# Two first part products of each single-row point placed ahead of the first softmax turns, the third ones behind

## The chip, the cores and the metric

The kernel runs on one core of one Trainium2 chip. The metric is the device time of one execution in microseconds (us), taken as the median of several runs.

## The reference, cut to what matters

The input `x` is four images of 256 channels by 64 by 64, in float32. Layer 0 computes 49 logits for every pixel, makes a softmax of them and uses the result as the weights of a 7x7 window with dilation 2. Layer 1 whitens the channels in four groups of 64 with statistics over all images.

```python
k = conv(x, w1, padding=6, rhs_dilation=2) + b1          # 128 channels, 7x7
k = conv(k, w2) + b2                                     # 49 logits per pixel
attn = softmax(k, axis=1)
shifts = stack([xp[:, :, 2*u:2*u+64, 2*v:2*v+64] for u in range(7) for v in range(7)])
x = einsum('bkchw,bkhw->bchw', shifts, attn)             # weighted 7x7 window
# layer 1: mean and covariance per group of 64 channels, five Newton steps for the
# inverse root, then the whitening matrix applied to the centred x, gain and shift
```

## The kernel before, in words

**The convolution.** The two convolutions of layer 0 are folded into one 7x7 filter bank with 49 outputs (`tap`). It is computed by interpolation in both directions: rows are taken in groups of four phases and combined at seven row points (`row_eval`), columns likewise at seven column points (`col_eval`), the products of one row point with all column points are matmuls (`conv_bank`, line 604) into two PSUM buffers `cv0` and `cv1` used in turn, and the results are interpolated back (`col_interp`, `row_interp`). Rows of one parity of one image lie in one of five SBUF slots, `slot0` to `slot4`. Logits of the first image lie in the first part of `slot4`.

Two of the seven row points, 0 and `INF`, need a single row phase, so their products may be made directly from the input with the seven column taps (`direct`, line 779, or in three part products). For the second image both points are made from three part products over pairs of columns (`direct_part`, line 862): part 2 uses the even taps, part 1 the odd taps, and part 3 uses sums of neighbouring taps on sums of neighbouring columns. `direct_sums` makes these sums on VectorE (line 345 is the helper that records every addition, lines 348 and 352 the ones for subtractions and multiply-adds), `direct_ends` joins the parts in `zz`: ScalarE copies part 1 (line 885), VectorE adds part 2 twice and subtracts the joined value from part 3. Point `INF` uses the PSUM buffers `acc0`, `acc1` and a `cv` buffer; point 0 uses two `cv` buffers and `acc0` (`direct_start`). Its taps are in the tile `lgx`, which later holds the weights of another row point (loaded by SyncE, line 426) and then logits.

**The weighted window of the first image.** `softmax(0, 0)` turns the logits by eight transposes on TensorE (line 1135), takes maxima on VectorE (line 1171), sixteen exponentials on ScalarE (line 1175), then scales and shuffles on VectorE (lines 1150 to 1159 and 1123). `move_terms` lets ScalarE copy the result into `zt` (line 1253) and GpSimd write it to DRAM (`sd`, line 1272). `load_band` lets SyncE read it back as a band matrix (`band`, line 1322). Then `weighted_sum` (line 1442) multiplies the band with turned blocks of the image (`xb`, transposes of line 1378). A second softmax, `softmax(0, 1)`, serves the other column parity.

**The order.** Each engine works through its own queue in order. A scheduler lays the instructions of each engine in an order from the program's order and priorities; during the first image the VectorE operations of the helpers are also chained one behind the other (`in_turn`, line 322). At the border between the images the program says

```python
    prepare(NR0, 0)                      # row and column point values of image 1
    xs, ws = direct_sums(1, INF, [w], gbr...)
    direct0(5, 1)
    row_interp(0, 1)                     # last logits of image 0
    direct_part(1, INF, 2, ...); direct_part(1, INF, 1, ...); direct_part(1, INF, 3, ...)
    prepare(NR0, 1); prepare(NR0, 2)
```

and then, for image 1, the steps `soft(0, 0)`, `direct_start(0)` (parts 2 and 1 of point 0), `direct_start(1)` (part 3 of point 0), `soft(0, 1)`, and the first `conv_step`s, which contain the first weighted sums at marked places.

Of the kernel before, what the change touches and what calls it, by code (L numbers as in the profile page):

```python
# [9 lines left out]
F32 = mybir.dt.float32  # L10
# [13 lines left out]
INF = 6  # L24
# [8 lines left out]
def kernel(  # L33
# [29 lines left out]
    nc = tc.nc  # L63
    B, C, H, W = x.shape
    P = 128
    NCC = C // P
    O1 = w1.shape[0]
    KT = w2.shape[0]
    KS = 7
# [12 lines left out]
    Q8 = SH // 4  # L82
# [23 lines left out]
    ps_y = ctx.enter_context(tc.tile_pool(name="ps_y", bufs=2, space=bass.MemoryType.PSUM))  # L106
# [74 lines left out]
    t = tp()  # L181
# [3 lines left out]
    t = tp()  # L185
# [5 lines left out]
    for k in range(2):  # L191
        t = ps_cv.tile([P, 512], F32, name=f"cv{k}")
# [8 lines left out]
    UPOS = {u: k for k, u in enumerate((6, 4, 5, 3, 2, 0, 1))}  # L201
    gpool = tc.alloc_tile_pool(name="gp", bufs=1, side="right")
    tap = gpool.tile([P, KS, KS, NCC, KT], F32, name="tap")
    gbr = gpool.tile([P, KS, NCC, 2, KT], F32, name="gbr")
# [33 lines left out]
    lgx = const.tile([P, max(SH * W, n3)], F32, name="lgx")  # L238
    gr0 = lgx[:, :n0].rearrange("p (v a s k) -> p v a s k", v=KS, a=NCC, s=2)
# [6 lines left out]
    for k, c0 in enumerate(range(0, P, CB)):  # L246
        n = min(CB, P - c0)
        t = cv_buf[k % 2]
# [15 lines left out]
    for k0 in range(0, KT, TB):  # L264
        n = min(TB, KT - k0)
        t = tp()
# [36 lines left out]
    spare = pv[:, NV - 1].rearrange("p n q b -> p (n q b)")  # L303
# [40 lines left out]
    def add(o, a, b):  # L344
        return in_turn(TT(o, a, b, ALU.add))  # L345
# [381 lines left out]
    def row_interp(b, part):  # L727

        pt = {k: zz[:K2, k] for k in range(NP)}
        lg = lgx  # L730
        if b == 0:
            lg = store[4].rearrange("p c r w -> p (c r w)")
        lg = lg[:, : SH * W].rearrange("p (r w) -> p r w", w=W)
        outs = phases(lg[:K2])
        cut = lambda t, k: t[:, k : k + Q8]
        tr = ct.rearrange("p a b -> p (a b)")[:K2, : Q9 * W].rearrange("p (q w) -> p q w", w=W)
        interpolate(pt, tr, outs, cut, part)
        if part == 0:
            done_ = ((0, outs[0]), (2, outs[2]))
        else:  # L740
            done_ = ((3, cut(pt[5], 0)), (1, outs[1]))
            logits[b] = lg
        for a, t in done_:

            def end(a=a, t=t):
                return nc.scalar.activation(outs[a], t, AF.Identity, bias=bias[:K2])

            if b > 0 and part == 0:
                later.append(end)
            else:  # L750
                end()
# [51 lines left out]

    M16, NX = W // 4, Q8 * 2 * NCC * W // 2

    def direct_sums(b, br, w, room):

        a = 3 if br == INF else 0
        xs = []
        for h in range(2):  # L810
            x = slots[2 * b + h].rearrange("p c r w -> p (c r w)").rearrange(
                "p (e a w) -> p a e w", a=4, w=SW
            )
            x = x[:, a].rearrange("p e (m i two) -> p i e m two", i=2, two=2)
            o = room[:, h * NX // 2 : (h + 1) * NX // 2]
            add(o.rearrange("p (e m two) -> p e m two", m=SW // 4, two=2), x[:, 0], x[:, 1])
            xs.append(
                o.rearrange("p (c g q w) -> p c g q w", c=NCC, g=2, q=Q8).rearrange(
                    "p c g q (m two) -> p c g q m two", two=2
                )  # L820
            )
        ws = []
        for s, t in enumerate(w):
            nw = (KS // 2) * NCC * KT
            o = room[:, NX + s * nw : NX + (s + 1) * nw]
            o = o.rearrange("p (v a k) -> p v a k", v=KS // 2, a=NCC)
            for j in range(KS // 2):
                add(o[:, j], t[2 * j + 1], t[2 * j])
            ws.append([o[:, j] for j in range(KS // 2)] + [t[KS - 1]])
        return xs, ws  # L830

    def direct_part(b, br, part, ps, w, xs=None):

# [42 lines left out]
    def direct_view(ps, n, m):  # L876
        return ps.rearrange("p q w -> p (q w)")[:, : n * m * 2].rearrange(
            "p (q m two) -> p q m two", q=n, two=2
        )

    def direct_ends(br, n, p1, p2, p3=None):

        z = zz[:K2, br, :n].rearrange("p q (m i two) -> p i q m two", i=2, two=2)
        if p3 is None:
            nc.scalar.copy(z[:, 0], p1[:K2])
            add(z[:, 1], z[:, 0], p2[:K2, :, 1:])
            add(z[:, 0], z[:, 0], p2[:K2, :, :M16])
        else:
            sub(z[:, 1], p3[:K2], z[:, 1])
# [3 lines left out]
    def conv_psum():  # L893
        ncv[0] += 1
        return cv_buf[(ncv[0] - 1) % 2].rearrange("p (q w) -> p q w", w=W)

    def direct_inf(b):
# [2 lines left out]
        t = spare[:, :NTAP].rearrange("p (v a k) -> p v a k", v=KS, a=NCC)  # L900
        direct(b, INF, 0, conv_psum(), [t[:, v] for v in range(KS)])

    start_of = {}

    def direct_start(sr):

        n = Q8 + 1
        w = [[gr0[:, v, :, s] for s in range(2)] for v in range(KS)]
        if sr == 0:
            room = store[4].rearrange("p c r w -> p (c r w)")[:, SH * W :]  # L910
            xs, ws = direct_sums(1, 0, [[t[s] for t in w] for s in range(2)], room)
            start_of["xs"] = xs
            start_of["ws"] = [[t[j] for t in ws] for j in range(KS // 2 + 1)]
            p2 = direct_view(conv_psum(), n, M16 + 1)
            direct_part(1, 0, 2, p2, w)
            p1 = direct_view(conv_psum(), n, M16)
            direct_part(1, 0, 1, p1, w)
            direct_ends(0, n, p1, p2)
        else:
            p3 = direct_view(acc[0], n, M16)  # L920
            direct_part(1, 0, 3, p3, start_of["ws"], start_of["xs"])
            direct_ends(0, n, None, None, p3)

    acc = [ps_y.tile([P, Q8, W], F32, tag="y", name=f"acc{sr}") for sr in range(2)]
    for a in acc:
        nc.vector.memset(a, 0.0)
    rows = [(0, br) for br in (1, 2, 3)]
    NR0 = len(rows)
    rows += [(b, br) for b in range(1, B) for br in ROWS if b > 1 or br]
# [41 lines left out]
    def direct0(br, sr):  # L971
        if br in xrs:
            gb = gb5 if br == 5 else gbr
            direct(
                0, br, sr, conv_psum() if br == 5 else acc[sr],
                [gb[:, v, :, sr] for v in range(KS)], xrs[br],
            )
        else:
            u = KS - 1 - 4 * sr - (3 if br == INF else 0)
            w = [tap[:, UPOS[u], v] for v in range(KS)]  # L980
            direct(0, br, sr, conv_psum() if br == INF else acc[sr], w)
# [92 lines left out]
    col_interp(0, 3)  # L1074
    row_interp(0, 0)
    prepare(NR0, 0)
    w = [tap[:, UPOS[3], v] for v in range(KS)]
    xs, ws = direct_sums(1, INF, [w], gbr.rearrange("p v a s k -> p (v a s k)"))
    direct0(5, 1)
    row_interp(0, 1)  # L1080

    w = [[t] for t in w]
    p2 = direct_view(acc[0], Q8, M16 + 1)
    direct_part(1, INF, 2, p2, w)
    p1 = direct_view(acc[1], Q8, M16)
    direct_part(1, INF, 1, p1, w)
    p3 = direct_view(conv_psum(), Q8, M16)
    direct_part(1, INF, 3, p3, [[t] for t in ws[0]], xs)
    prepare(NR0, 1)
    prepare(NR0, 2)  # L1090
    strict[0] = False
    direct_ends(INF, Q8, p1, p2)
    direct_ends(INF, Q8, None, None, p3)
    gpool.release()


# [563 lines left out]
    def soft(b, pc):  # L1660
        steps = softmax(b, pc)

        def step():
            with tc.high_priority() if pc == 0 else nullcontext():
                next(steps, None)

        step()
        if b == 0:
            step()
            if pc == 0:  # L1670
                bands(0)
        else:
            rest_of.append(step)
# [32 lines left out]
    for b in range(1, B):  # L1706

        steps = []
        for k, (bk, br) in enumerate(rows):
            if bk == b:  # L1710
                for i, cost in enumerate((6, 5, 2)):
                    steps.append((cost, lambda k=k, i=i: conv_step(k, i)))
        if b == 1:
            for sr in range(2):
                steps.insert(sr, (12, lambda sr=sr: direct_start(sr)))
            steps.insert(0, (0, lambda: soft(0, 0)))
            steps.insert(3, (0, lambda: soft(0, 1)))
        else:
            steps.insert(0, (12, lambda b=b: direct_inf(b)))
        j, at, whole = 0, 0, sum(c for c, _ in steps)  # L1720
        for cost, f in steps:
            half_next[0] = (at + cost) * NPC >= (j + 1) * whole and (b, j) in half_gaps
            f()
            while rest_of:
                rest_of.pop()()
            at += cost
            if at * NPC >= (j + 1) * whole:
                gap(b, j)
                j += 1
                while after_gap:  # L1730
                    after_gap.pop()()
# [26 lines left out]
    n = 4 * last_b  # L1758
# [186 lines left out]
    pair = bank_pairs()  # L1945
# [88 lines left out]
```

## Time and profile before

| | |
|---|---|
| median of 3 runs | 668.89 us (668.85 to 669.1) |
| the profiled execution | 668.98 us |
| its span in the trace | 667.2 us |
| TensorE (PE) busy | 638.7 us, 96% |
| VectorE (DVE) busy | 571.2 us, 86% |
| ScalarE (ACT) busy | 331.8 us, 50% |
| GpSimd (POOL) busy | 115.3 us, 17% |
| mean granted TensorE clock | 0.991 |

The profile has one execution. A busy time counts instructions on an engine. The chain of waits follows the work that ended last back to the beginning, step by step, to what released it. In rows of the timeline the first column is the start, the second the busy time, `x` the number of instructions, and a bracket holds the idle time just before and what ended it. Consecutive instructions overlap a little at their ends, so the distance from one start to the next is shorter than the busy time of one.

### The profile page before, as it was taken

How to read it: one execution, taken by the hardware profiler on the slowest of the kernel's cores; microseconds unless marked ns; L12 is line 12 of the kernel's file. 1: busy time of each engine (PE TensorE's matmuls, PEld its weight loads, DVE VectorE, ACT ScalarE, POOL GpSimd, SP SyncE). 2: the span in 40 equal slices, each digit the busy share in tenths (PEclk: the TensorE clock that was granted, in tenths of full speed). 3: DMA queues.
4: the chain of work that ended last, by engine and by line, in shares of the span. 5: the costliest groups of instructions: out<-in, count | busy, mean ns of one | idle time of the engine just before them, and what ended most of it. 6: DMA issues, size and time to landing. Idle time of an engine off the chain costs nothing.

```text
span 667.2 us, 19415 instructions
## 1 busy us (share of the span) xinstructions
PE 638.7 (96%) x7992; PEld 530.1 (79%) x7992; DVE 571.2 (86%) x1258; ACT 331.8 (50%) x861; POOL 115.3 (17%) x173
## 2 busy tenths in 40 slices
PE   6999999999999999999999999999999999999991
PEld 1439673358999998889999998999999999997440
DVE  3699999999899889999999799989999988634781
ACT  1434331013565566467754554473855667535681
POOL 0000551663213002001022020002220203500000
PEclk9999999999999999999999999999999999999996
DMA  8961799995599988324588673026364325739698
GB/s 316 247 177 67 128 232 382 218 195 83 133 205 223 228 257 304 103 57 108 149 278 278 232 246 107 1 69 195 103 197 112 70 65 129 182 96 380 263 412 335
DMA packets 109840, 126.11 MB, mean 189 GB/s; under 512 B 69127, under 2 KB 92216, under 8 KB 107576
## 3 DMA queue, kind: packets, MB, share of 16 engines
q1 hardware_dynamic: 92952, 69.35, 35.5%
q0 software_dynamic: 10752, 37.26, 21.7%
q10 hardware_dynamic: 6048, 18.27, 8.8%
q8 instruction: 63, 1.03, 0.7%
q14 instruction: 25, 0.20, 0.1%
HBM read 78.78 MB, written 52.36 MB: 197 GB/s over the span
## 4 chain that ended last, share of the span: by engine, by line
PE 62%; DVE 17%; issue 7%; POOL 4%; SPq 4%; DMA 3%; ACT 2%; DVEq 0%; ACTq 0%; POOLq 0%
PE cv L604 25%; PE y L1442 13%; PE sig L1533 5%; PE tp L1514 4%; PE tp L1378 4%; SPq L225 4%; POOL ahead L147 2%; POOL slot L147 2%; PE tp L1844 2%; PE cv L862 2%; DVE zz L352 2%; DVE rb L345 2%; PE cv L779 2%; DVE xh L352 2%; DVE pv L352 1%
## 5 line engine op out<-in xcount | busy, mean ns | idle before, releaser
L604 PE MATMUL cv<-xh,wr 128*49 128x128 f32 x4160 | 232.3, 273 | 0.1
L604 PEld LDWEIGHTS cv<-xh,wr 128*49 128x49 f32 x4160 | 226.2, 124 | 2.9 <-issue 1.0
L1272 POOL DMA_DIRECT2D sd<-zt x120 | 63.3, 534 | 292.2 <-ACT zt L1253 222.2
L1442 PE MATMUL y<-band,xb 128*128 128x209 f32 x448 | 93.7, 341 | 0.6 <-ACT xb L1409 0.6
L1442 PEld LDWEIGHTS y<-band,xb 128*128 128x128 f32 x448 | 75.7, 191 | 1.5 <-ACT xb L1409 0.8
L615 ACT COPY pv<-cv 113x486 f32<-113x486 f32 (+2 forms) x60 | 25.9, 431 | 82.4 <-PE cv L604 82.2
L352 DVE SCALAR_TENSOR_TENSOR pv<-pv 113x162 f32<-113x162 f32 x176 | 52.5, 320 | 1.5 <-ACT pv L615 1.0
L1524 ACT COPY yt<-tp 128x512 f32<-128x512 f32 x60 | 35.0, 591 | 24.3 <-PE tp L1514 23.5
L1253 ACT COPY zt<-d 32x112 f32<-32x112 f32 (+2 forms) x132 | 38.6, 293 | 11.0 <-DVE d L1123 5.1
L1514 PE MATMUL tp<-ident,slot 128*128 128x128 f32 x240 | 41.3, 295 | 0.2 <-ACT slot L1464 0.2
L1378 PE MATMUL tp<-ident,slot 128*128 128x128 f32 x256 | 40.5, 282 | 0.0
L1175 ACT ACTIVATE d<-tp,mx 128x49 f32<-128x49 f32 x96 | 27.4, 321 | 24.2 <-DVE mx L1172 17.6
L1533 PE MATMUL sig<-yt 128*64 128x65 f32 x1024 | 38.0, 225 | 0.9 <-ACT yt L1524 0.9
L1514 PEld LDWEIGHTS tp<-ident,slot 128*128 128x128 f32 x240 | 34.9, 205 | 5.0 <-issue 3.7
L1378 PEld LDWEIGHTS tp<-ident,slot 128*128 128x128 f32 x256 | 38.2, 204 | 0.2 <-issue 0.2
L1533 PEld LDWEIGHTS sig<-yt 128*64 128x64 f32 x1024 | 32.9, 137 | 6.7 <-issue 1.9
L1409 ACT COPY xb<-tp 128x512 f32<-128x512 f32 x52 | 30.6, 588 | 13.7 <-PE tp L1378 10.5
L352 DVE SCALAR_TENSOR_TENSOR xh<-ct 128x512 f32<-128x512 f32 x40 | 26.6, 691 | 5.7 <-PE cv L604 5.4
L147 POOL DMA_DIRECT2D slot<-in_x_dram x12 | 20.4, 1701 | 53.4 <-DVE xh L352 38.6
L348 DVE TENSOR_TENSOR pv<-pv 113x162 f32<-113x162 f32 (+1 forms) x77 | 27.5, 364 | 0.3
L352 DVE SCALAR_TENSOR_TENSOR xh<-xh,rb 128x512 f32<-128x512 f32 x40 | 27.4, 684 | 0.1
L345 DVE TENSOR_TENSOR ct<-rb 128x1024 f32<-128x1024 f32 (+1 forms) x26 | 26.5, 1020 | 0.3
(288 smaller groups left out, 1141.9 us busy)
## 6 DMA issues: line engine op xcount, KB each, us to landing
band<-sd SPq DMA_DIRECT2D x64, 242.0 KB, 3.6
sd<-zt POOLq DMA_DIRECT2D x120, 77.0 KB, 4.2
wr<-gd ACTq DMA_DIRECT2D x14, 588.0 KB, 4.8
wr<-gd ACTq DMA_DIRECT2D x14, 490.0 KB, 4.1
slot<-in_x_dram POOLq DMA_DIRECT2D x12, 512.0 KB, 10.5
ahead<-in_x_dram POOLq DMA_DIRECT2D x12, 512.0 KB, 7.8
spill<-slot POOLq DMA_DIRECT2D x3, 2048.0 KB, 9.4
slot<-ahead POOLq DMA_DIRECT2D x3, 2048.0 KB, 10.7
```

Of the source, the lines that this page charges most:

```text
L147: yield queue.dma_start(o[:, cc, h], src[:, :, pr, h * SW : (h + 1) * SW])
L345: return in_turn(TT(o, a, b, ALU.add))
L352: return in_turn(STT(o, a, f, b, ALU.mult, ALU.add))
L604: nc.tensor.matmul(o, wv[:, sc, sr, cc], xv[bc][:, h * NCC + cc], start=(j == 0), stop=(j == len(terms) - 1), skip_group_check=True,)
L1253: ins = nc.scalar.copy(o, i)
L1272: dma = queue.dma_start(bass.AP(tensor=D.tensor, offset=D.offset + h * HS + g * RS, ap=[[LS, TC], [CR * RS, NCH], [1, KS * WS]],), zt[p0 : ...
L1378: nc.tensor.transpose(t[:, h * C + cc * P : h * C + (cc + 1) * P], tile_of(xt, cc, t8, h, pc), turned_by(n),)
L1409: (nc.vector.tensor_copy if n > 4 * B - 3 else nc.scalar.copy)(xb.rearrange("p a c -> p (a c)"), t[:, : 2 * C])
L1442: nc.tensor.matmul(y_ps[n, half, cc][:, q0 : q0 + nq, c0:c1], xb[:, cc * P : (cc + 1) * P], rhs, start=(k == 0), stop=(k == len(PIECES[hal ...
L1514: nc.tensor.transpose(t[:, h * C + cc * P : h * C + (cc + 1) * P], tile_of(yt, cc, t8, h, pc), turned_by(n),)
L1524: return nc.scalar.copy(yb.rearrange("p h a g c -> p (h a g) c")[:, :, :GW], t[:, : 2 * C].rearrange("p (e c) -> p e c", c=GW),)
L1533: nc.tensor.matmul(sig[g * GW : (g + 1) * GW, cc], yb[:, g, :GW], yb[:, g], start=(count[0] == 0), stop=end, skip_group_check=True,)
```

## The change

The three part products of `INF` are taken apart: parts 2 and 1 are joined as soon as they are made, part 3 is made in `direct_start(1)`, just ahead of part 3 of point 0. `direct_start(0)` now stands ahead of `soft(0, 0)`. Point 0's part 3 goes to `acc1` instead of `acc0`, so one `cv` buffer less is drawn and the two change places from there on. The column sums of `INF` go to `spare` (a part of `pv`), its tap sums and a copy of its last tap (ScalarE) to the free end of `lgx`. The sums of the taps are made in one addition over all of them, where there were three for `INF` and six for point 0.

```diff
+        return xs, direct_taps(w, sums)
+
+    def direct_taps(w, sums):
+        n = w.shape[2]
+        o = sums[:, : KS // 2 * n].rearrange("p (v n) -> p v n", n=n)
+        pair = w[:, : KS - 1].rearrange("p (v two) n -> p two v n", two=2)
+        add(o, pair[:, 1], pair[:, 0])
+        return [o[:, j] for j in range(KS // 2)] + [w[:, KS - 1]]
...
         else:
-            p3 = direct_view(acc[0], n, M16)
+            third_inf()
+            p3 = direct_view(acc[1], n, M16)
             direct_part(1, 0, 3, p3, start_of["ws"], start_of["xs"])
             direct_ends(0, n, None, None, p3)
+    def third_inf():
+        p3 = direct_view(acc[0], Q8, M16)
+        direct_part(1, INF, 3, p3, start_of["ws_inf"], start_of["xs_inf"])
+        direct_ends(INF, Q8, None, None, p3)
...
     prepare(NR0, 0)
-    w = [tap[:, UPOS[3], v] for v in range(KS)]
-    xs, ws = direct_sums(1, INF, [w], gbr.rearrange("p v a s k -> p (v a s k)"))
     direct0(5, 1)
+    p2 = direct_view(acc[0], Q8, M16 + 1)
+    direct_part(1, INF, 2, p2, [one(g[:, v]) for v in range(KS)])
+    p1 = direct_view(acc[1], Q8, M16)
+    direct_part(1, INF, 1, p1, [one(g[:, v]) for v in range(KS)])
     row_interp(0, 1)
-    w = [[t] for t in w]
-    p2 = direct_view(acc[0], Q8, M16 + 1)
-    direct_part(1, INF, 2, p2, w)
-    p1 = direct_view(acc[1], Q8, M16)
-    direct_part(1, INF, 1, p1, w)
-    p3 = direct_view(conv_psum(), Q8, M16)
-    direct_part(1, INF, 3, p3, [[t] for t in ws[0]], xs)
+    direct_ends(INF, Q8, p1, p2)
+    room = lgx[:, 2 * KS * NCC * KT :]
+    start_of["xs_inf"], ws = direct_sums(1, INF, g, spare, room)
     prepare(NR0, 1)
     prepare(NR0, 2)
     strict[0] = False
-    direct_ends(INF, Q8, p1, p2)
-    direct_ends(INF, Q8, None, None, p3)
+    last_tap = room[:, KS // 2 * NCC * KT :][:, : NCC * KT]
+    nc.scalar.copy(last_tap, g[:, KS - 1])
...
             for sr in range(2):
                 steps.insert(sr, (12, lambda sr=sr: direct_start(sr)))
-            steps.insert(0, (0, lambda: soft(0, 0)))
+            steps.insert(1, (0, lambda: soft(0, 0)))
             steps.insert(3, (0, lambda: soft(0, 1)))
```

## The prediction

> **What bounds the kernel now.** I read the page first: the engines, then the shares of the chain that ended last.
>
> ```profile
> PE 638.7 (96%) x7992; PEld 530.1 (79%) x7992; DVE 571.2 (86%) x1258; ACT 331.8 (50%) x861; POOL 115.3 (17%) x173
> PE 62%; DVE 17%; issue 7%; POOL 4%; SPq 4%; DMA 3%; ACT 2%; DVEq 0%; ACTq 0%; POOLq 0%
> ```
>
> PE is nearly always busy, so only PE idle time can be won. Next, PE's waits from 150 to 320 us: two lie in the changed stretch.
>
> ```profile
> PE tp L1135 <- ACT slot L746: 1.6, 1, 1.6
> PE cv L862 <- DVE gbr L345: 0.9, 1, 0.9
> ```
>
> The first is the turn of the first logits, the second the third product of `INF`, waiting for its sums. Then the chain of waits from 140 to 215 us:
>
> ```profile
> 154.16 0.73 ACT slot L746
> 154.89 0.04 issue
> 154.94 1.21 PE tp L1135 x8
> 156.15 12.56 PE cv L862 x218
> 168.71 6.56 PE acc L862 x128
> 175.27 0.68 PE tp L1378 x4
> 175.95 0.95 PE tp L1135 x8
> 176.90 9.74 PE cv L604 x176
> 186.64 0.91 PE y L1442 x4
> ```
>
> From the turns to the first weighted sum (line 1442, starting at 186.57 in the timeline) PE never waits, and the chain stays on PE to 247 us. But the sum also needs the band, so I followed the band in the timelines of DVE, ACT and SP:
>
> ```profile
> 149.74 0.61 DVE L345 TENSOR_TENSOR zz<-zz,cv 113x448 f32<-113x448 f32 x1
> 155.91 1.03 DVE L1171 TENSOR_REDUCE mx<-tp 128x8 f32<-128x392 f32 x2
> 166.84 3.33 ACT L1253 COPY zt<-d 128x56 f32<-128x56 f32 x11 [5.11 <-DVE d L1123]
> 176.94 0.91 SPq L1322 DMA_DIRECT2D band<-sd x2
> 176.45 1.05 DVE L1171 TENSOR_REDUCE mx<-tp 128x8 f32<-128x392 f32 x2 [0.16 <-PE tp L1135]
> ```
>
> Maxima begin at 155.91 and the band load at 176.94, which is 21.0 us of latency. The load's issues to landing are 3.65 us, so the band is there at 180.6: 6.0 us of slack before 186.57. The last row shows the other thing to see: DVE's first stop of any size after 140 us is at 176.3. Until then it works without a pause, so an operation's time there is its place in DVE's queue.
>
> **The change on PE.** `INF`'s first two parts end at 148.86 as before. Point 0's parts 2 and 1 need only taps and input, so they follow at once: 148.86 + 12.56 = 161.4. The logits are ready long before, so the turns take 0.95 (row 175.95, without the idle start): 162.4. `INF`'s third part takes 3.5 (149.80 to 153.29 in PE's timeline): 165.9. Point 0's third 6.56: 172.4. Transposes and second turns 0.68 + 0.95, convolution 9.74: PE stands before the first weighted sum at 183.8. That is 2.8 us earlier than 186.57: the waits of 0.94 and 1.65 and 0.26 of the idle start. This is the whole gain on offer.
>
> **The change on DVE.** In the changed program's queue the maxima of the first softmax no longer follow the last logit operations; the sums for the third parts and much of the next rows' preparation stand ahead. From 148.02, where DVE began `INF`'s column sums, the queue now holds, by start-to-start distances of the same rows before:
> - last logits, from the `zz` addition to the last multiply-add into the logits (149.74 to 154.05): 4.3
> - the two additions of part 2 of `INF`: 2 x 0.4 = 0.8
> - `INF`'s column sums: 1.2 (148.02 to 149.23); its tap sums, one addition of 294 elements, like 113x288 (0.36 to 0.45): 0.4
> - `ct` and the `xh` of two banks (1.25, 0.61, 0.60, 0.72, 1.34): 4.5
> - point 0's column sums: 1.2; its tap sums, one addition of 588, like 113x576 (0.67 to 0.76): 0.7
> - `rb` 2.20, `rb` 1.13, `ct` 1.14: 4.5
>
> The sum is 17.6, so the maxima begin at 165.6 against 155.91: 9.7 later, though their turns are ready at 162.4. The single tap additions save about 0.1 for `INF` (0.51 for three) and 0.4 for point 0 (six at 0.17 to 0.25); this is in the sum.
>
> **The band.** After the maxima come the exponentials, 1.2 later, for 4.6, at 171.4. Meanwhile DVE does `zz` additions, three `rb` steps of 1.14 and the subtraction of `INF`'s third part. That subtraction is a new wait on PE ahead of the reciprocals, hence ahead of the whole band; its product ends at 165.9 and DVE reaches it at 169.6, so it costs nothing, and would cost only what the product ran past 169.6. Reciprocals to shuffles take 1.7 after the exponentials (184.01 against 182.3 in the second softmax; 1.87 in the first). So the shift shrinks to 9.5. Copies, GpSimd's writes and SyncE's load follow as before (10.1 us from the first copy to the load): load at 186.45, landed at 190.1. **PE, ready at 183.8, waits 6.3 us and starts the sum at 190.1 instead of 186.57: +3.5.** The gain of 2.8 is turned into a wait.
>
> **Queues passed.** On SP the load of `spare` (126.54 before) now waits for `INF`'s third product, 165.9, and stands ahead of the `lgx` load (175.32 before, now 172.4) and the band: both go before 186.45, cost 0. ACT's copy of part 1 stands ahead of the exponentials: done at 161.9, needed at 166.8, cost 0; without that cover it is 0.43. The copy of the last tap, 98 elements, lies before 130 us, where ACT is mostly idle: 0, at most 0.3. POOL keeps its order. On ACT the second softmax's sixteen exponentials, behind the late `zt` copies, run 180.1 to 184.8 instead of 177.67 to 182.3, and DVE waits for them about 4 us. What is queued behind on DVE (`xh`, `pv`) then ends near 195; the next `xh` needs the convolution behind the weighted sums, which ends at 197, so the delayed sums hide it.
>
> **Landing.** Two weight loads (588 and 490 KB, ACT queue) now start at about 184.8 and 185.4, just ahead of the band. Band loads took 2.4 to 8.1 us over the trace, median 3.6; the next pair, issued with a weight load beside it, took 7.5. I take 3.65, because the first pair had the 686 KB load of `lgx` 1.6 us ahead of it as well. The bounds are -1.2 and +4.5.
>
> **The clock.** No idle time of 6 us inside this trace shows its price. The end does: PE's last matmul ends at 652.85, and the windows table (the clock is the third number from the right) gives
>
> ```profile
> 652.00:654.00 2.00, 0.85 (x8) 0.00 (x0) 1.54 (x2) 1.58 (x3) 0.00 (x0) 1.00 0.99 401
> 654.00:656.00 2.00, 0.00 (x0) 0.00 (x0) 0.00 (x0) 0.00 (x0) 0.00 (x0) 0.90 0.98 410
> 656.00:658.00 2.00, 0.00 (x0) 0.00 (x0) 0.00 (x0) 0.00 (x0) 0.00 (x0) 0.50 1.06 442
> ```
>
> A mean of 0.90 over 2 us is full clock until 655.6, then half: the clock falls about 2.75 us after the last matmul. An idle time of 6.3 us should see it fall. How long it stays low afterwards no row shows. It cannot gain; at most the first weighted sums and their transposes (186.57 to 191.5) run at half rate, +5.0. I take the fall time for the return too: 2.75 us at half rate lose 1.4. The Trainium skill, TensorE: Matmul & The Clock Gate, Part 1, speaks against a change that opens such a gap: it halves the clock after an idle window of about 3.4 us and restores it after about as long a busy one. By that page, as an estimate, the loss would be 1.7 instead of 1.4.
>
> **Sum.** +3.5 + 1.4 = +4.9, all on PE's chain, which passes it on: to 247 us the chain is PE, then DVE released by PE (its waits there name `PE cv L604`), then PE again. The profiled execution took 668.98 us (span 667.2 and 1.8 around it), 0.09 above the median. 668.98 + 4.9, rounded: 673.9.
>
> **Rivals.** (1) The band is hidden and PE's gaps are simply closed: 668.98 - 2.8 = 666.2. It needs the band shifted by no more than 183.8 - 180.6 = 3.2 us; the turns alone come 162.4 - 156.15 = 6.3 later, which speaks against it. 5%. (2) DVE does not hold the maxima back (its queue runs shorter than the rows): the shift is that of the turns, 6.3 to 6.5, the band lands at 187.0, and PE starts 0.5 later than before, with an idle time of 3.2 at the edge of the clock's fall: 669.5, no change. It decides if DVE reaches the maxima by 162.5; 17.6 us of rows would have to shrink by 3. 9%. (3) The band lands in 7.5 beside the weight loads: +3.85 more, 677.8. 15%. (4) The clock does not fall, or returns at once: +3.5, 672.5; I count it to the forecast's range.
>
> **How the numbers follow.** Forecast with (4): 71%. Its own bounds are an early landing without clock loss (+2.3, 671.3) and a somewhat late landing with a longer clock loss (about +7, 676). With (3) the range is 671.0 to 677.8; left out below are (1) and (2), 14%. This kernel's measurement can tell 0.2%, 1.3 us, from no change. Faster: (1) and a little of (2), 6%. Same: the rest of (2), 8%. Slower: 86%.
>
> **What would show it.** Right: maxima at about 165.6, band load near 186.5, PE idle about 6 us before the first sum, the wait named after the band's DMA, and a granted clock under 1 in that stretch. Wrong: maxima right behind the turns at 162.5; a first sum at 184; or a later stretch, 247 to 290 us, taking the shift back.

## The result, and the profile after

| | before | after |
|---|---|---|
| median | 669.0 us (668.85 to 669.21, 4 runs) | 675.83 us (674.79 to 676.81, 4 runs) |
| ratio | | 1.0102, 95% interval 1.0086 to 1.0118 |
| profiled execution, span | 668.98, 667.2 us | 676.81, 675.0 us |

The changed kernel is 6.8 us slower. The profiled execution of it is the longest of the four; a second trace, shown below, has 674.87 us. Of the 39 runs of the kernel before in the two series of the experiments' table, 24 lie from 668.7 to 669.5 us and 15 from 670.4 to 671.4, and only an execution of the lower group was traced. In the fences below, line numbers from the softmax on are 12 higher than before: 1135 is now 1147, 1171 is 1183, 1253 is 1265, 1322 is 1334, 1442 is 1454.

The page of after, engines and the shares of the chain that ended last:

```profile
PE 641.5 (95%) x7992; PEld 532.8 (79%) x7992; DVE 571.0 (85%) x1251; ACT 332.2 (49%) x862; POOL 115.1 (17%) x173
PE 72%; DVE 16%; ACT 4%; issue 3%; DMA 3%; POOL 0%; SPq 0%; ACTq 0%; DVEq 0%; POOLq 0%
```

PE has as many matmuls as before, yet 2.8 us more busy time: some of them ran slowly. PE's waits have lost the two rows for the first turns (1.6) and for `gbr` (0.9), and gained one:

```profile
PE y L1454 <- DVE xh L352: 6.9, 1, 6.9
```

PE's timeline of after (start, duration, line, operation, and in brackets the idle time before it):

```profile
148.62 12.59 PE L862 MATMUL cv<-slot,lgx 128*49 128x128 f32 x224
161.14 1.21 PE L1147 MATMUL tp<-ident,slot 113*128 113x113 f32 x8
162.29 3.49 PE L862 MATMUL acc<-pv,lgx 128*49 128x128 f32 x64
173.89 9.81 PE L604 MATMUL cv<-xh,wr 128*49 128x128 f32 x176
190.62 1.73 PE L1454 MATMUL y<-band,xb 128*128 128x209 f32 x4 [6.91 <-DVE xh L352]
198.40 11.56 PE L604 MATMUL cv<-xh,wr 128*49 128x128 f32 x208
```

The gaps before the weighted sum are gone, PE is through at 183.7, and then it stands for 6.91 us. The sum starts at 190.62, 4.05 later than before. The next convolution starts at 198.40 against 191.53, 6.87 later: between the two the five pieces of the first weighted sums and their transposes took 7.78 us instead of 4.96. The two rows of before for this comparison:

```profile
186.57 0.98 PE L1442 MATMUL y<-band,xb 128*128 128x209 f32 x4
191.53 11.56 PE L604 MATMUL cv<-xh,wr 128*49 128x128 f32 x208
```

The timelines of DVE, ACT and SP of after give the way to the band:

```profile
165.49 1.03 DVE L1183 TENSOR_REDUCE mx<-tp 128x8 f32<-128x392 f32 x2
176.45 3.33 ACT L1265 COPY zt<-d 128x56 f32<-128x56 f32 x11 [5.12 <-DVE d L1135]
185.16 1.83 SPq L1334 DMA_DIRECT2D band<-sd  x2
184.68 0.49 DVE L1162 RECIPROCAL s<-s 128x8 f32<-128x8 f32 x2 [4.46 <-ACT d L1187]
```

Maxima at 165.49, the band's load at 185.16, 8.2 later than before. The loads of the two pairs landed 3.1 to 5.3 us after their issue (median 4.2), the first one after 5.3; 185.16 + 5.3 = 190.5, and PE starts at 190.62. The profile names an `xh` step of VectorE as what PE waited for, and that step ends at 190.55; the second trace, below, shows that PE does not need it. The windows of after (the clock is the third number from the right) show why the pieces were slow:

```profile
184.00:186.00 2.00, 0.00 (x0) 0.00 (x0) 1.24 (x6) 1.90 (x10) 0.00 (x0) 1.00 1.00 188
186.00:188.00 2.00, 0.00 (x0) 0.00 (x0) 1.96 (x7) 0.00 (x0) 0.00 (x0) 0.63 0.85 294
192.00:194.00 2.00, 2.00 (x9) 1.85 (x8) 1.93 (x8) 0.73 (x2) 0.00 (x0) 0.50 1.03 231
196.00:198.00 2.00, 2.00 (x13) 1.98 (x12) 0.00 (x0) 1.02 (x3) 0.00 (x0) 0.81 0.99 137
198.00:200.00 2.00, 2.00 (x34) 1.88 (x35) 0.00 (x0) 2.00 (x4) 0.00 (x0) 1.00 1.43 149
```

A mean of 0.63 over 186 to 188 is full clock until 186.5, 2.8 us after the last matmul; 0.81 over 196 to 198 is half clock until 196.8, 6.1 us after PE's restart.

### The profile page after: what moved, and what is told of

The parts are those of the page before. It is cut to its first block, busy times and chain, and to the rows that moved or that the text cites. A ratio compares the mean times of both kernels' runs of the same rounds, so it can differ in the third digit from the quotient of the medians.

```text
span 675.0 us, 19410 instructions
## 1 busy us (share of the span) xinstructions
PE 641.5 (95%) x7992; PEld 532.8 (79%) x7992; DVE 571.0 (85%) x1251; ACT 332.2 (49%) x862; POOL 115.1 (17%) x173
## 4 chain that ended last, share of the span: by engine, by line
PE 72%; DVE 16%; ACT 4%; issue 3%; DMA 3%; POOL 0%; SPq 0%; ACTq 0%; DVEq 0%; POOLq 0%
PE cv L604 29%; PE y L1454 13%; PE acc L779 7%; PE sig L1545 4%; PE tp L1526 4%; PE cv L779 3%; PE tp L1390 3%; PE cv L251 2%; PE tp L1856 2%; DVE zz L352 2%; DVE pv L352 1%; ACT d L1187 1%; PE cv L1856 1%; DVE xh L352 1%; PE apply L1856 1%
## 5 line engine op out<-in xcount | busy, mean ns | idle before, releaser
L1454 PE MATMUL y<-band,xb 128*128 128x209 f32 x448 | 95.9, 347 | 7.7 <-DVE xh L352 6.9
L1454 PEld LDWEIGHTS y<-band,xb 128*128 128x128 f32 x448 | 77.6, 195 | 8.9 <-issue 7.5
L352 DVE SCALAR_TENSOR_TENSOR rb<-slot 128x1024 f32<-128x1024 f32 (+1 forms) x26 | 26.9, 1057 | 0.0
## 6 DMA issues: line engine op xcount, KB each, us to landing
slot<-in_x_dram POOLq DMA_DIRECT2D x12, 512.0 KB, 10.1
```

Of the source, the lines that this page charges most:

```text
L352: return in_turn(STT(o, a, f, b, ALU.mult, ALU.add))
L1454: nc.tensor.matmul(y_ps[n, half, cc][:, q0 : q0 + nq, c0:c1], xb[:, cc * P : (cc + 1) * P], rhs, start=(k == 0), stop=(k == len(PIECES[hal ...
```

## The experiments

The theory: **the turns' new place delays the band; VectorE's queue adds to that; TensorE runs out of work, stands until the band has landed, and the idle time halves its clock for a while.** The rivals: the turns' delay alone, `INF`'s third product and its sums, or the tap sums do the harm. Totals are medians, ratios are against the kernel before in the same series, where that kernel's runs lay from 668.69 to 671.38 us.

| kernel | median (runs), us | ratio, 95% interval |
|---|---|---|
| order only | 678.07 (677.2 to 679.29) | 1.0132 (1.0111 to 1.0154) |
| turns first | 672.98 (672.46 to 673.54) | 1.0056 (1.0041 to 1.0071) |
| softmax first | 669.49 (667.69 to 674.54) | 1.0008 (0.9987 to 1.0028) |
| no idle, 56 | 679.45 (679.11 to 679.88) | 1.0153 (1.0138 to 1.0168) |
| no idle, 28 | 674.18 (674.09 to 674.83) | 1.0067 (1.0052 to 1.0083) |
| tap sums | 669.01 (668.66 to 669.29) | 0.9986 (0.9976 to 0.9996) |
| turns between | 667.59 (667.12 to 668.32) | 0.9965 (0.9954 to 0.9976) |
| turns between, softmax first | 671.77 (666.14 to 674.91) | 1.0015 (0.9991 to 1.0039) |

**Order only.** The kernel before, with this edit alone:

```
-            steps.insert(0, (0, lambda: soft(0, 0)))
+            steps.insert(1, (0, lambda: soft(0, 0)))
```

> The kernel before with one edit alone: the turns of the first image's row-0 logits come behind point 0's two parts instead of ahead of them. INF's three products stay where they were, and the tap sums too. My theory: the turns run at about 166.8 and the maxima at about 169, some 13 us later than in the kernel before; the band is loaded at about 189 and lands at 193 to 194, TensorE idles 7 to 8 us from 186 and the clock falls: first weighted sum 7 us later, 2.8 us of slow clock, 677 to 679 us. Rival: the harm of the change comes from what INF's third product and its sums displaced, not from the turns: 671 us or less.

678.07 us, as expected. Its timelines of DVE, SP and PE:

```profile
168.94 1.03 DVE L1171 TENSOR_REDUCE mx<-tp 128x8 f32<-128x392 f32 x2
189.06 2.55 SPq L1322 DMA_DIRECT2D band<-sd  x2
193.38 1.73 PE L1442 MATMUL y<-band,xb 128*128 128x209 f32 x4 [7.77 <-DMA band<-sd]
```

Maxima 13.0 us later than before, band load 12.1 later, first sum 6.8 later, and the five pieces in 7.11 us: 2.15 lost to the clock, which came back 4.7 us after the restart. This one edit does more harm than the whole change; `INF`'s third product behind, which lets the turns come 5.2 us sooner than here, takes some of it back. The rival is out.

**Turns first.** The changed kernel, with the turns back ahead of point 0's parts:

```
-            steps.insert(1, (0, lambda: soft(0, 0)))
+            steps.insert(0, (0, lambda: soft(0, 0)))
```

> The changed kernel, with the turns of the first image's row-0 logits put back ahead of point 0's parts; INF's third product stays behind, the tap sums stay as changed. My theory: the cost of the change is the first weighted sum's start, which the turns' new place sets through VectorE's maxima, shuffles and the band load. Here TensorE has nothing between the INF parts' end at 148.6 and the logits, which land near 153.2, so it idles some 4.5 us there; its own queue then runs without a stop to 188.4, with the maxima at about 157.5 and the band long landed. First weighted sum near 188.4 instead of 190.6 (before: 186.6); 1.8 us over before by the start alone, up to 2.8 more if the clock falls in the 4.5 us and the parts pay for it: 670.8 to 673.6 us. Rival: the late turns are the only cost, the rest of the change (INF's third product behind, one addition for the tap sums) costs nothing: 669.0 us or less.

672.98 us, inside the theory's range and over the rival's 669.0. PE's timeline of it:

```profile
153.19 1.78 PE L1147 MATMUL tp<-ident,slot 113*128 113x113 f32 x8 [4.35 <-ACT slot L746]
154.90 14.48 PE L862 MATMUL cv<-slot,lgx 128*49 128x128 f32 x224
190.52 0.98 PE L1454 MATMUL y<-band,xb 128*128 128x209 f32 x4
```

One of its windows, with the clock third from the right:

```profile
158.00:160.00 2.00, 2.00 (x32) 1.98 (x30) 1.97 (x4) 2.00 (x16) 2.00 (x5) 0.77 0.05 10
```

The idle time is now before the turns, for the logits, with the band loaded at 179.76 and no wait at the sum. PE's own queue ends 2.1 us later than the 188.4 expected from the idle time alone, since the clock fell 3.3 us after the last matmul and was half until 158.9, 5.7 us after the restart: turns and parts took 16.0 us instead of the changed kernel's 13.7. So the changed kernel's order does cover the logits' lateness, and an idle time of 4.35 us in another place costs its clock as well.

**Softmax first.** The changed kernel; VectorE's chained helper work is hung on the last shuffle of the first softmax (`shuffle` returns its last instruction):

```
+        ins = shuffle(d.rearrange("p h i (u v) -> p (h i u) v", u=KS))
+        if (b, pc) == (0, 0):
+            turn[0] = ins.ins.name
```

> The changed kernel, with VectorE's chained helper work tied behind the first softmax's shuffles instead of wherever it fell, so that it cannot stand between the turns and the maxima. TensorE's order is the changed one. My theory: the turns end at 162.2 and the maxima then follow within a microsecond instead of 3.3 us later, the band is loaded at 182 to 183 instead of 185.2, lands near 187, and TensorE idles some 3.3 us instead of 6.9; if that is too short for the clock to fall, the 2.8 us of the slow clock go too: 669.4 to 670.5 us, up to 672 if the clock still falls. Rival: the late turns alone (or a busier DMA queue at that time) set the band's landing, VectorE's queue plays no part: 675 us, idle time still near 7 us.

669.49 us, 6.3 less than the changed kernel with the same order of PE. Its DVE, SP and PE rows:

```profile
161.99 1.03 DVE L1184 TENSOR_REDUCE mx<-tp 128x8 f32<-128x392 f32 x2
181.42 0.91 SPq L1337 DMA_DIRECT2D band<-sd  x2
185.42 0.95 PE L1457 MATMUL y<-band,xb 128*128 128x209 f32 x4 [1.82 <-DMA band<-sd]
```

Maxima 3.5 us sooner than in the changed kernel (165.49), load 3.7 sooner, and with only 1.82 us idle the clock stayed at 1.00. VectorE's queue is thus a needed part of the cause, not a detail: the turns' place without it (this kernel) costs nothing that these runs can tell, 0.3% at most by the interval. The total lies where the theory had it; the idle time is 1.5 us shorter than it said, and the traced run took 668.24 us. One of ten runs took 674.54 us with a mean clock of 0.986 (the traced run 0.991); it was not traced.

**No idle, 56 matmuls.** The changed kernel, and ahead of the first weighted sum:

```
+        if (n, half, k) == (0, 0, 0):
+            idle = tp()
+            for _ in range(56):
+                pe(nc.tensor.matmul(idle[:, :P], ident, ident, start=True, stop=True,
+                                    skip_group_check=True))
```

> The changed kernel with 56 more matmuls of 128 columns ahead of the first weighted sum, which multiply the identity by itself into a buffer that nobody reads (some 6.3 us at 0.11 us each): TensorE is busy while it waits for the band. My theory: the first weighted sum still starts near 190.6, since the band sets it, but the clock stays at 1.00 and the first five pieces take about 5.0 us as before the change instead of 7.8: 2.8 us less than the changed kernel, 673.0 us. Rival: the slow clock costs nothing, because the pieces wait for their bands and copies anyway: 675.8 us.

679.45 us: a miss, by the size of the filler. Its row reads

```profile
183.54 12.77 PE L1444 MATMUL tp<-ident 128*128 128x128 f32 x112
```

Each of the 56 shows as two passes of 0.114 us, so that the filler ran until 196.3, past the band. It still told the price of the pieces at full clock: from 196.15 to the convolution at 200.92, 4.77 us.

**No idle, 28 matmuls.** The same with half the number.

> The changed kernel with 28 more matmuls of 128 columns ahead of the first weighted sum, identity by identity into a buffer that nobody reads. The earlier run with 56 of them showed that each counts as two passes of 0.114 us, so that 28 fill 6.4 us, from 183.6 to 190. My theory: the first weighted sum starts near 190.6 as in the changed kernel, the clock stays at 1.00, and the five pieces take 4.8 us as in the run with 56 instead of 7.8: 3.0 us less than the changed kernel, 672.5 to 673.0 us, and a spread between runs of well under 2 us. Rival: the slow clock costs nothing behind the first sum, or the extra matmuls hold others up: 675.8 us or more.

674.18 us, 1.65 less than the changed kernel, between theory and rival. PE's rows:

```profile
183.76 6.52 PE L1444 MATMUL tp<-ident 128*128 128x128 f32 x56
192.65 0.95 PE L1463 MATMUL y<-band,xb 128*128 128x209 f32 x4 [2.37 <-DVE pv L349]
197.50 11.56 PE L605 MATMUL cv<-xh,wr 128*49 128x128 f32 x208
```

The clock stayed at 1.00 in every window and the pieces took 4.85 us, 2.93 less than the 7.78: that part held. But the sum started 2.03 later than in the changed kernel, because the band's first load, issued at 185.50, landed only 7.0 us later instead of 5.3 (185.50 + 7.0 = 192.5). DVE's rows stood within 0.2 us of the changed kernel's, where PE started before this `pv` step, so the wait is for the band here too, whatever operation the profile names: `xh` in one trace, `pv` in this one. In the run with 56 matmuls the same load took 5.8 us. Why it takes longer is open.

**Tap sums.** The kernel before, with each set of tap sums in one addition:

```
-            for j in range(KS // 2):
-                add(o[:, j], t[2 * j + 1], t[2 * j])
+        add(o, pair[:, 1], pair[:, 0])
```

> The kernel before with one edit alone: each set of tap sums in one addition instead of three per share. All orders stay. My theory: this removes some VectorE additions of 0.1 to 0.2 us each, which lie in time that VectorE has to spare except behind the INF sums, where TensorE waited 0.94 us for the row-part's sums: 668.0 to 669.0 us, at most 0.2% from the kernel before. Rival: the one larger addition ends later than the first of the small ones, and delays the third product that waits for its first tap: up to 1 us slower, 670 us.

669.01 us; the interval ends at 0.9996, within the 0.2% that the measurement can tell, and 669.01 is 0.1 us from the 668.89 that the kernel before took at the start. No effect on the time to see, as both the theory and the prediction had it. VectorE's order did not quite stay, though: an `rb` step of 2.29 us now stands ahead of the first softmax's shuffles, which begin at 166.33 instead of 163.60, and the band is loaded at 180.51 instead of 176.94. The first sum starts at 186.66 all the same, so a delay of the load by 3.6 us is seen to fit into the slack of 6.0.

**Turns between.** The changed kernel, with the turns between point 0's two parts:

```
             direct_part(1, 0, 2, p2, w)
+            soft(0, 0)
             p1 = direct_view(conv_psum(), n, M16)
...
-            steps.insert(1, (0, lambda: soft(0, 0)))
-            steps.insert(3, (0, lambda: soft(0, 1)))
+            steps.insert(2, (0, lambda: soft(0, 1)))
```

> As the other kernel with the turns between point 0's two parts, but VectorE's helper work chained as in the changed kernel. My theory: TensorE's order is the same, VectorE may hold the maxima some 2 to 3 us (to about 159), the band is loaded at about 180 and lands at about 184: first weighted sum at 183.7 to 185, 666.2 to 667.8 us. If VectorE's order decides also here: later by what its queue holds the maxima beyond 159. Rival: with the turns ahead of part 1 VectorE's queue plays no part, same time as the other within 0.3 us.

667.59 us, faster than the kernel before (ratio 0.9965; it is 1.4 us or 0.2% under the 669.0 of the first table), and the best steady version of all. Rows of PE, DVE, SP:

```profile
148.68 7.29 PE L862 MATMUL cv<-slot,lgx 128*49 128x128 f32 x128
155.91 1.21 PE L1148 MATMUL tp<-ident,slot 113*128 113x113 f32 x8
159.20 1.03 DVE L1184 TENSOR_REDUCE mx<-tp 128x8 f32<-128x392 f32 x2
180.77 0.90 SPq L1335 DMA_DIRECT2D band<-sd  x2
185.34 0.95 PE L1455 MATMUL y<-band,xb 128*128 128x209 f32 x4 [1.59 <-DMA band<-sd]
```

The 7.29 us behind 148.68 cover the logits, the turns come 1.0 us later than in the kernel before, and of the 2.8 us of closed gaps PE keeps 1.2: it is ready at 183.7 and still waits 1.59 us for the band. Its span is 665.9 against 667.2.

**Turns between, softmax first.** Both edits.

> The changed kernel with two edits: the turns of the first image's row-0 logits stand between point 0's two parts (behind part 2, ahead of part 1), and VectorE's chained helper work is tied behind the first softmax's shuffles. My theory: part 2 covers the 4.4 us that the logits are late, so TensorE does not idle at 148.6; the turns end at about 156.1, the maxima follow at about 156.6, the band is loaded at about 177 and has landed by 181, ahead of TensorE's own end at 183.6. The first weighted sum then starts at 183.7 to 184, which is 2.7 to 2.9 us earlier than in the kernel before, with no idle time and a full clock: 666.0 to 666.4 us. Rival: the 2.8 us of closed gaps are given back behind the first sum, where bands, copies and the next pieces' loads have not moved: 668 to 669 us.

The first sum did start at 183.72, 2.85 earlier than before, with no idle time: that part of the theory held. The way to it did not: `ct` and `xh` steps of VectorE still stood ahead of the maxima, which began at 159.22 (156.6 expected; 159.20 with the one edit), and the band was loaded at 179.53 instead of 177. The median of 671.77 us did not hold with the theory either, and it is beyond the rival's 668 to 669 too; the twelve runs lay from 666.14 to 674.91. The rows of PE, ACT and SP near 256 us in the traced run (672.13 us):

```profile
262.20 0.86 PE L1458 MATMUL y<-bandz,xbz 128*128 128x96 f32 x4 [4.98 <-ACT xbz L1416]
260.35 1.04 ACT L510 COPY rb<-slot 128x1024 f32<-128x1024 f32 x1 [4.10 <-DMA slot<-in_x_dram]
244.63 0.58 SPq L147 DMA_DIRECT2D slot<-in_x_dram  x1
```

ScalarE's copy of an image tile waits 4.10 us for its load, and behind it in ScalarE's queue stand the edge copies that the sum needs. The load was issued at 244.63; in the kernel before the same issue is at 239.60, with the turns between alone at 242.29, in both ScalarE does not wait for the load, and PE's wait at this place is 1.10. Here the clock fell to 0.64 in 262 to 264 and to 0.50 after. A second trace was taken of this kernel:

> The kernel with the turns between point 0's two parts and VectorE's helper work behind the first softmax, once more, for a second trace of it. In the first trace the 2.7 us gained at the first weighted sum were lost at 256 us, where ScalarE's copy of an image tile waited 4.10 us for its load and the edge copies stood behind it. My theory: the time of a run is decided by that load. A run near 666 to 667 us shows no wait of ScalarE for the image tile near 256 us and a TensorE wait of about 1.1 us there, as in the kernel before; a run near 672 us shows 4 to 5 us of it again. Rival: the runs differ in the first weighted sum's start (183.7 us or later) or in the clock there: then the start differs and the wait at 256 us does not.

671.51 us, with first sum at 183.56, issue at 245.46, ScalarE's wait 2.94, PE's 3.83, and the clock at 0.67 and 0.50 again. What goes wrong is shown twice; that the runs near 666 us lack this wait is likely but was not seen. The SP timelines show where its queue fell back: the batch of four image loads began at 187.60 instead of 182.91, behind band loads that had gone later, and ended issuing at 204.7 instead of 197.25. Why the batch itself took 17.1 us instead of 14.3 stays open.

**The changed kernel once more.**

> The changed kernel once more, for a second trace of it: how far the first weighted sum's start and the clock's return belong to one execution. My theory: VectorE's queue and with it the band's load repeat within 0.3 us (185.0 to 185.5); the landing (5.3 us before, 7.2 us in the run with 28 extra matmuls) and the time at which the clock returns (6.2 us after the restart) vary, by 2 us together: first weighted sum at 189.5 to 192.7, total 674 to 677.5 us. Rival: both repeat within 0.3 us, and the spread between the runs lies behind 200 us.

674.87 us. PE's and SP's rows:

```profile
185.61 1.45 SPq L1334 DMA_DIRECT2D band<-sd  x2
190.24 1.73 PE L1454 MATMUL y<-band,xb 128*128 128x209 f32 x4 [6.48 <-DMA band<-sd]
196.93 8.29 PE L604 MATMUL cv<-xh,wr 128*49 128x128 f32 x148
```

Two of its windows, with the clock third from the right:

```profile
186.00:188.00 2.00, 0.00 (x0) 0.00 (x0) 1.96 (x7) 0.00 (x0) 0.00 (x0) 0.82 0.89 276
194.00:196.00 2.00, 2.00 (x14) 1.99 (x13) 0.83 (x4) 1.46 (x4) 0.00 (x0) 0.97 1.55 172
```

The load repeats within 0.45 us, a little more than expected; landing and clock vary more. This time the wait bears the band's name, and the `xh` step that the first trace names ends here at 190.59, after PE's start at 190.24: PE does not need it. The pieces took 6.69 us, 1.73 over before, and the clock fell at 187.3 and returned at 194.1, 3.9 us after the restart (first trace: 2.82 over before, and 6.1). The two traces differ by 1.47 us at that convolution and by 1.9 in the span, so most of their difference lies before 200 us. The rival is out.

## Why the prediction was right, and where not

The forecast was 673.9 us, in 671.0 to 677.8; it came out at 675.83, slower, and by the mechanism named. Point by point:

- **PE through at 183.8, 2.8 earlier.** Measured 183.70 and 183.75 in the two traces. In the version with the turns between the parts, 1.2 of this reaches the end of the run.
- **Maxima at 165.6 by DVE's queue.** Measured 165.49 and 165.56. The sum of 17.6 us from rows of before was good to 0.1, and the softmax-first kernel shows that the queue is what matters. Rival (2), 669.5 us, is about the kernel that this experiment built, and that took 669.49; the match to 0.01 is luck, since the rival had the first sum 0.5 us later than before, and its trace has it 1.15 us earlier, in a run of 668.24 us.
- **Later softmax.** DVE's stop before the second reciprocals was 4.46 us (about 4 foreseen), and no later wait on PE is put down to it.
- **Band load at 186.45, landed at 190.1.** Two errors nearly cancel, and that is luck. The copies into `zt` began at 176.45 and 176.50, as worked out (166.84 + 9.5 = 176.3), but from there to the load it took 8.7 and 9.1 us instead of 10.1, so the load went at 185.16 and 185.61, about 1 us earlier; and it landed in 5.3 and 4.5 us instead of 3.65. The first sum at 190.62 and 190.24 is 4.05 and 3.67 later than before, where 3.5 was forecast. Rival (3), 7.5 us of landing, was not what happened, though the run with 28 filler matmuls had 7.0.
- **The clock: +1.4. This is the step that failed in size.** The fall, 2.75 us after the last matmul, was read rightly from the end of the trace (2.8 measured, 3.5 in the second trace). For the return no row existed, and taking the same 2.75 us was too short: 6.1 and 3.9 us, and the cost 2.82 and 1.73. The run with 28 filler matmuls, where the clock never fell in this stretch, confirms the price, 2.93 us. A fixed delay, as the prediction took it for both switches, is not what the traces show: the switches lie on a grid in time (last section), so that 2.8 for the fall was in part luck too.
- **Nothing is taken back later, nothing added.** Half right: the shift was not taken back, but it grew. In the second trace it is 5.40 at the next convolution, 5.68 at 293.97 (the wait for `xb` there is 0.85 instead of 0.57), and 5.97 at 614.24. This term of 0.5 to 0.9 us was missing from the sum.
- **The wait's name.** It was to be named after the band's DMA; the first trace names `DVE xh`, the second the DMA.

The sum for the second trace, 3.67 + 1.73 + 0.5, is 5.9, its span's excess; for the first 4.05 + 2.82 + 0.9 is 7.8. The forecast had 3.5 + 1.4.

The Trainium skill, TensorE: Matmul & The Clock Gate, Part 1, bears on the failed step with a sentence that the prediction left out: the window in which the gate judges PE is free-running, and so the number of slow matmuls differs between runs. If a whole window of about 3.4 us must be busy, the return lies one to two windows after the restart, 3.4 to 6.8 us as an estimate from that page. The six returns measured here, 3.8, 3.9, 4.5, 4.7, 5.7 and 6.1, all lie within it. The prediction's use of the page, 3.4 us, took the lower end for the whole.

## What to carry to other kernels

Where work is moved ahead of a step that starts a long chain of small operations and transfers, cost the chain's start on every engine's queue, not on the one whose gaps are to be closed: here the same order of PE costs 1% or nothing according to what stands on VectorE. Half of the work ahead was enough to cover the late input; putting the turns after the first part instead of both gives 667.59 us. An idle time of TensorE that lets the clock fall costs more than itself, and a chain made earlier can find the next transfer not yet there.

## What was not expected of the hardware

- **The clock's return varies.** Half clock lasted 3.9 and 6.1 us after the restart in two executions of one program, 4.7 and 5.7 us in two others, 3.8 and 4.5 us in the two traces with both edits; waits of 1.6, 1.8 and 2.4 us did not make it fall, and one of 3.8 and longer ones did. The fall came 2.3 to 3.5 us after the last matmul in four of these stretches. Near 257 us in the two traces with both edits it came 5.4 and 4.9 us after it, when PE had already been at work again for 0.4 and 1.1 us.
- **The switches lie on a grid.** In each of these six traces the fall, the return and the fall behind the last matmul of the kernel lie whole multiples of 3.413 us apart, to 0.03 us: in the first trace of after they are at 186.52, 196.76 (3 steps) and 664.38 (137 more). Behind the first 10 us of the traces, a step of this grid in which PE was busy for a third or less was followed by half clock, and with 43% or more full clock was kept; at half clock a step 80% busy did not bring full clock back, and each step busy throughout did. So what a wait costs depends on where the grid lies against it.
- **One load's landing varies between executions that treat it alike:** the first band load of the first sum, at nearly the same time behind the same work, took 4.5, 5.3, 5.8 and 7.0 us.
- **A filler matmul in f32 of 128 columns shows as two passes** of 0.114 us each.
